# A four-layer graph network on one core: other instructions for the sorted neighbours' weighted sums and for the neighbour lists, one fused step in layer 1, and gathers tied to VectorE's progress

## Chip, core and metric

The kernel runs on one core of a Trainium2 chip, as one program. The metric is the device time of one execution in microseconds (us). The engines are named as in the profile: PE is TensorE, DVE is VectorE, ACT is ScalarE, POOL is GpSimd, and SP issues most of the DMAs.

## What is computed

Sixteen graphs of 1024 nodes, each with a 1024 x 1024 matrix `adj` of edge weights (about 1.6% of them nonzero) and 64 features per node, go through four residual layers. Each begins with a layer norm and a ReLU.

```python
h = max(layernorm(x), 0); x = x + (tanh([h, adj @ h] @ W1 + b1) @ W2 + b2)     # layer 0
h = max(layernorm(x), 0); num = (adj + I) @ h; den = rowsum(adj + I)           # layer 1
x = x + where(isnan(num / den), 0, num / den)
h = max(layernorm(x), 0); valid = dilated(adj) > 0                             # layer 2
agg[n, c] = sum over (tau, w) of w * quantile(h[valid[n], c], tau)             # tau .25 .5 .75
x = x + mask * (relu((h + agg) @ W1 + b1) @ W2)
h = max(layernorm(x), 0); x = x + ((adj @ h) / deg) @ Wn + h @ Ws + bias       # layer 3
```

Layer 2 is the hard one: for each node and each of the 64 features, three interpolated quantiles over the node's own ragged set of neighbours (some 10 to 38 of them).

## The kernel before

Everything is done graph by graph, with the 128 partitions holding nodes, eight blocks of 128 nodes per graph. Six Python generators, called streams, each walk over the 16 graphs and issue their instructions piece by piece:

- `adjacency`: loads `adj`, transposes it on PE, marks nonzero entries (L872, L874), takes out the dilated ones and writes for each node a row of keys to DRAM, 1024 minus the column for each neighbour and 0 elsewhere. It also sorts the nodes by how many neighbours they have. Ten of its PE and ACT steps wait for one another.
- `layers`: layers 0 and 1 and the layer norm of layer 2 (`messages` at L843 is the product `adj @ h` on PE, copied out by ACT at L844; layer 1's division is at L1118 to L1127).
- `neighbour_lists`: POOL loads the key rows of the nodes in order of their neighbour count (L1017, an indirect DMA). DVE takes the eight largest keys of each row with MAX8 (L1034), blanks them out with MATCH_REPLACE8 (L1037), takes the next eight, and so on: 22 MAX8 and 14 MATCH_REPLACE8 per graph. The found keys become the indices of the neighbours (L1043). It also works out weights `wts`, one for each sorted place of each node.
- `gathers`: for every place in a node's list POOL issues one indirect DMA that brings the 256-byte feature row of that neighbour (L1154), 152 of them per graph into five tiles `raw0` to `raw4`.
- `sorts`: DVE sorts the gathered rows place against place with a pruned network of minima and maxima between `raw` and a second tile `other` (L1190), then multiplies the places that can hold a quantile by their weights (L1207) and adds them with a strided reduction (L1211). The result `agg` goes to DRAM.
- `tail`: POOL brings `agg` back in the nodes' order (L1228), then the rest of layer 2 and layer 3 follow.

The eight blocks of nodes form five groups by neighbour count (`GROUPS`): two groups of one block with up to 38 and 20 places, and three groups of two blocks with up to 18, 16 and 13. The tiles `raw0` to `raw4` have one buffer each, so the gathers of a group for one graph start when the same group of the graph before is sorted. The lists run one graph ahead of the sorts.

The order of all instructions is written out by a planner: a variable `clk.dve` advances by a cost that the code states for each piece, each stream yields the time at which its next piece may start, and the loop takes the first stream that is due. Each engine executes its instructions in the resulting order. DVE counts its finished instructions in a semaphore. An instruction that nobody waits for leaves its count to a later one, so that a run of several sorting steps is posted by one addition at its last step.

Of the kernel before, what the change touches and what calls it, by code (L numbers as in the profile page):

```python
# [7 lines left out]
F32 = mybir.dt.float32  # L8
F16 = mybir.dt.float16
BF = mybir.dt.bfloat16  # L10
I32 = mybir.dt.int32
U16 = mybir.dt.uint16
# [6 lines left out]
C = 64  # L19
# [11 lines left out]
B_SW, B_SW2, B_LB, B_END = 0, 252, 504, 3576  # L31
H_ID, H_OFF, H_ONE, H_G, H_PI, H_END = 0, 128, 256, 384, 516, 1028

GROUPS = [(0, 1, 38, 17), (1, 1, 20, 15), (2, 2, 18, 12), (4, 2, 16, 10), (6, 2, 13, 1)]

E_ID, E_ONE, E_CAP, E_LOW, E_CN, E_Q, E_END = 0, 128, 256, 264, 272, 280, 320
J_ID, J_BIG, J_OFF, J_ST, J_ROW, J_ONE, J_PI, J_NI, J_END = 0, 128, 256, 384, 1408, 2432, 2560, 2688, 2696
KB = 4  # L40


# [665 lines left out]
def direct_path(ctx: ExitStack, tc: tile.TileContext, t: dict, out: bass.AP, flag):  # L708
# [24 lines left out]
    identf, onesf = cf[:, E_ID:E_ID + P], cf[:, E_ONE:E_ONE + P]  # L733
    cap8, low8, cn8 = (cf[:, e:e + NB] for e in (E_CAP, E_LOW, E_CN))
    identh, big_i, offdiag = (ch[:, e:e + P] for e in (J_ID, J_BIG, J_OFF))
    stair, pidx = ch[:, J_ST:J_ST + N], ch[:, J_PI:J_PI + P]
    nid = ch[:, J_NI:J_NI + NB]
    jrow, onerow = ch[0:1, J_ROW:J_ROW + N], ch[0:1, J_ONE:J_ONE + P]
    eps = const.tile([P, 1], F32, name="eps")
# [25 lines left out]
    w3n, w3s = weight("L3_gnn_W_neighbors", C), weight("L3_gnn_W_self", C)  # L765
    b3 = along("b3", t["L3_gnn_bias"])

    mask8 = const.tile([B * NB, P], U8, name="mask8")
    nc.gpsimd.dma_start(mask8, nodemask.rearrange("b (i p) -> (b i) p", p=P))
    maskf = const.tile([B * NB, P], F32, name="maskf")  # L770
    nc.vector.tensor_copy(maskf, mask8)
    pm = psum.tile([P, 512], F32, tag="t", name="pt", bufs=3)
    nc.tensor.transpose(pm[:, :B * NB], maskf, identf[:B * NB, :B * NB])
# [31 lines left out]
    def mid(u, shape):  # L805

        return work.tile(shape, F32, tag=f"mid{u}", name="mid", bufs=2)
# [38 lines left out]
    def per_node(p, lhs, w):  # L846

        for i in range(NB):
            nc.tensor.matmul(p[:, i * C:(i + 1) * C], lhs[:, i * P:(i + 1) * P], w, start=True, stop=True)  # L849
        return p.rearrange("p (i c) -> p i c", c=C)  # L850


    state = [dict() for _ in range(B)]
# [154 lines left out]
    def neighbour_lists(b):  # L1008


        g = state[b]
        ks = []

        def load_keys(i):
            if i < NB:
                k = lists.tile([P, N], F16, name="k", bufs=KB)
                nc.gpsimd.indirect_dma_start(k, None, g["keys_d"],  # L1017
                                             bass.IndirectOffsetOnAxis(ap=g["node"][:, i:i + 1], axis=0))
                clk.pool = max(clk.pool, clk.dve) + 1.3
                ks.append((k, clk.pool + 3.5))  # L1020

        for i in range(KB):
            load_keys(i)
        total = sum(n * -(-cap // 8) * 8 for _, n, cap, _ in GROUPS)
        found = lists.tile([P, total], F16, name="found", bufs=1)
        m = g["m"]
        o = 0
        for b0, n, cap, _ in GROUPS:
            for i in range(b0, b0 + n):
                src, at = ks[i]  # L1030
                yield at
                for r in range(-(-cap // 8)):
                    e = found[:, o:o + 8]
                    nc.vector.max(out=e, in_=src)  # L1034
                    clk.dve += 1.2
                    if (r + 1) * 8 < cap:
                        nc.vector.match_replace(out=src, in_to_replace=e, in_values=src, imm_value=0.0)  # L1037
                        clk.dve += 1.3
                    o += 8
                    yield clk.dve  # L1040
                load_keys(i + KB)
        index = lists.tile([P, total], I32, name="index")
        ts(index, found, -1.0, float(N), op0=ALU.mult, op1=ALU.add)  # L1043

        s = nodes.tile([P, 2, NB], F32, name="s")
        tt(s[:, 0], m, cap8, ALU.is_gt)
        tt(s[:, 1], m, low8, ALU.is_lt)
        tt(s[:, 0], s[:, 0], s[:, 1], ALU.max)
        tt(bad, bad, s[:, 0], ALU.max)

        at = nodes.tile([P, 3, NB], F32, name="at")
        for k in range(3):
            ts(at[:, k], m, (k + 1) / 4, -(k + 1) / 4, op0=ALU.mult, op1=ALU.add)
# [12 lines left out]
        g.update(index=index)  # L1066
        done.add(("index", b))
        yield after(1.7, act=1.7)
        wts = lists.tile([P, QT], F32, name="wts", bufs=3)
        tt(wts, far[:, 0], far[:, 2], ALU.add)  # L1070
        tt(wts, wts, far[:, 1], ALU.add)
        clk.dve += 0.4
        g.update(wts=wts)
        done.add(("lists", b))


    def layers(b):
# [39 lines left out]
        den = nodes.tile([P, NB, 1], F32, name="den")  # L1117
        ts(den, p[:, :, C:C + 1], 1.0, None, op0=ALU.add)  # L1118
        nc.vector.reciprocal(den, den)
        o, o1 = mid(0, [P, NB, C]), mid(0, [P, NB, C])  # L1120
        tt(o, p[:, :, :C], ha[:, :, :C], ALU.add)
        tt(o, o, den.to_broadcast([P, NB, C]), ALU.mult)

        ts(o1, o, 0.0, None, op0=ALU.max)
        ts(o, o, 0.0, None, op0=ALU.min)
        tt(o, o, o1, ALU.add)
        tt(x, x, o, ALU.add)  # L1127
        clk.dve += 3.8
        ha = nodes.tile([P, NB, C + 1], F32, name="h2", bufs=3)
        yield from preln(0, x, ha)  # L1130
        nc.sync.dma_start(h_ds[b % 3][:N].rearrange("(i p) c -> p i c", p=P), ha[:, :, :C])
# [10 lines left out]
    def gathers(b):  # L1142
        g = state[b]
        yield max(g["rows_at"], clk.pool)
        for k, (b0, n, cap, _) in enumerate(GROUPS):
            while not (b == 0 or ("sort", b - 1, k) in done):
                yield None
            raw = raws.tile([P, cap, n * C], F32, name=f"raw{k}")
            o = sum(c * -(-r // 8) * 8 for _, c, r, _ in GROUPS[:k])
            clk.pool = max(clk.pool, clk.dve)  # L1150
            for s in range(cap):
                for i in range(n):
                    at = o + i * -(-cap // 8) * 8 + s
                    nc.gpsimd.indirect_dma_start(raw[:, s, i * C:(i + 1) * C], None, h_ds[b % 3],  # L1154
                                                 bass.IndirectOffsetOnAxis(ap=g["index"][:, at:at + 1], axis=0))
                clk.pool += 1.27 * n
                if s % 4 == 3:
                    yield clk.pool - 3
            g[f"raw{k}"] = (raw, clk.pool + 4)
            done.add(("gather", b, k))  # L1160
        done.add(("gathers", b))


    def view(v, first, dims, w):

# [6 lines left out]
    def sorts(b):  # L1172
# [3 lines left out]
        for k, (b0, n, cap, low) in enumerate(GROUPS):  # L1176
# [20 lines left out]
            q = hi + 1 - lo  # L1197
            o = sum((_span(kk, ll)[1] + 1 - _span(kk, ll)[0]) * m for _, m, kk, ll in GROUPS[:k])
            wv = g["wts"][:, o:o + q * n].rearrange("p (q i) -> p q i", i=n)
            for (s, _, i, j), dims in result:  # L1200
                (c, d, _), outer = dims[-1], dims[0] if len(dims) > 1 else (1, 0, 0)
                d = max(d, 1)
                for r in range(outer[0]):
                    fr, to = i + r * outer[1], j + r * outer[1]
                    for ii in range(n):
                        cols = slice(ii * C, (ii + 1) * C)
                        tt(raw[:, fr:fr + (c - 1) * d + 1:d, cols], two[s][:, fr:fr + (c - 1) * d + 1:d, cols],  # L1207
                           wv[:, to:to + (c - 1) * d + 1:d, ii:ii + 1].to_broadcast([P, c, C]), ALU.mult)
                        clk.dve += 0.085 + c * C / 960
                        yield clk.dve  # L1210
            nc.vector.tensor_reduce(agg[:, b0:b0 + n].rearrange("p i c -> p (i c)"),  # L1211
                                    raw[:, lo:hi + 1].rearrange("p q w -> p w q"), AX.X, ALU.add)
            clk.dve += 0.085 + q * w / 960
            done.add(("sort", b, k))
            yield clk.dve
        yield clk.dve + 2
# [99 lines left out]
    with tc.manual_schedule():  # L1316
        ready = [0.0] * len(streams)
        while streams:

            soonest = None  # L1320
            for k, at in enumerate(ready):
                if at is not None and at > clk.dve:
                    soonest = at if soonest is None else min(at, soonest)
                    continue
                said = next(streams[k], -1.0)
                if said == -1.0:
                    del streams[k], ready[k]
                    break
                ready[k] = said
                if said is not None:  # L1330
                    break
            else:
                assert soonest is not None
                clk.dve = soonest
# [19 lines left out]
def _constants():  # L1354
# [14 lines left out]
    eh[p, J_BIG + p] = 2048  # L1369
    eh[:, J_OFF:J_OFF + P] = 1  # L1370
    eh[p, J_OFF + p] = 0
    eh[:, J_ST:J_ST + N] = p[:, None] < np.arange(N)
    eh[p, J_ST + p] = 2050
    eh[0, J_ROW:J_ROW + N] = -1024 - np.arange(N)
    eh[0, J_ONE:J_ONE + P] = 1
# [76 lines left out]
```

## Time and profile before

| | |
|---|---|
| median of 9 executions | 5327.71 us (5291.95 to 5380.86) |
| the profiled execution: its time, its span | 5354.12 us, 5352.3 us |
| granted TensorE clock | 0.637 |
| DVE busy | 3641.1 us, 68% of the span, 8698 instructions |
| POOL busy | 2830.9 us, 53%, 2707 instructions |
| PE busy | 2170.4 us, 41% |
| ACT busy | 1413.8 us, 26% |
| DMA | 372.65 MB, of which 117.88 MB by POOL's indirect DMAs |

Busy time says how long an engine had an instruction in it. On DVE independent instructions overlap a little, so the sum over instructions is larger than the time that they take in a row; start-to-start times from the timeline are the safer measure. In the waits "remote" and "issue" mark idle time for whose end the profile names no instruction.

### The profile page before, as it was taken

How to read it: one execution, taken by the hardware profiler on the slowest of the kernel's cores; microseconds unless marked ns; L12 is line 12 of the kernel's file. 1: busy time of each engine (PE TensorE's matmuls, PEld its weight loads, DVE VectorE, ACT ScalarE, POOL GpSimd, SP SyncE). 2: the span in 40 equal slices, each digit the busy share in tenths (PEclk: the TensorE clock that was granted, in tenths of full speed). 3: DMA queues.
4: the chain of work that ended last, by engine and by line, in shares of the span. 5: the costliest groups of instructions: out<-in, count | busy, mean ns of one | idle time of the engine just before them, and what ended most of it. 6: DMA issues, size and time to landing. Idle time of an engine off the chain costs nothing.

```text
span 5352.3 us, 33205 instructions
## 1 busy us (share of the span) xinstructions
PE 2170.4 (41%) x8387; PEld 1024.2 (19%) x8387; DVE 3641.1 (68%) x8698; ACT 1413.8 (26%) x2594; POOL 2830.9 (53%) x2707
## 2 busy tenths in 40 slices
PE   6443215444343435534344443434434353552022
PEld 3221112121211212121121211112121221211011
DVE  2445768756766677766767776776877766776755
ACT  5332213222322223232222322222232322321000
POOL 0436365664566566545655465564546555554740
PEclk8666656666565666656666666666766666665555
DMA  3322323332333434233332334333233432423221
GB/s 101 64 82 47 70 55 71 93 58 63 85 63 81 69 78 84 49 86 64 85 67 49 102 56 98 63 81 67 64 91 56 98 61 67 65 55 71 42 43 40
DMA packets 251851, 372.65 MB, mean 70 GB/s; under 512 B 120160, under 2 KB 120352, under 8 KB 251648
## 3 DMA queue, kind: packets, MB, share of 16 engines
q0 software_dynamic: 92640, 117.88, 18.3%
q1 hardware_dynamic: 158864, 251.87, 14.0%
q8 instruction: 68, 1.11, 0.1%
q14 instruction: 135, 1.11, 0.1%
q10 hardware_dynamic: 144, 0.69, 0.0%
HBM read 256.97 MB, written 113.25 MB: 69 GB/s over the span
## 4 chain that ended last, share of the span: by engine, by line
DVE 42%; another core or an unknown queue 27%; issue 12%; PE 10%; ACT 7%; DMA 2%; POOL 0%; SPq 0%; DVEq 0%; ACTq 0%; POOLq 0%
DVE other L1190 11%; DVE raw L1190 10%; DVE found L1034 6%; DVE k L1037 4%; DVE raw L1207 2%; PE pt L843 2%; PE pt L849 1%; ACT nb L885 1%; ACT nb L954 1%; PE tm L1272 1%; DVE agg L1211 1%; DVE nb L872 1%; PE pt L920 1%; ACT pt L956 1%
## 5 line engine op out<-in xcount | busy, mean ns | idle before, releaser
L1154 POOL DMA_INDIRECT raw<-h_d,index x2432 | 2540.5, 1045 | 1453.8 <-issue 724.4
L1190 DVE TENSOR_TENSOR other<-raw 128x128 f32<-128x128 f32 (+7 forms) x1488 | 764.4, 532 | 164.7 <-remote 104.3
L1190 DVE TENSOR_TENSOR raw<-other 128x256 f32<-128x256 f32 (+10 forms) x1424 | 676.7, 489 | 26.1 <-remote 12.7
L843 PE MATMUL pt<-adjt,ha 128*65 128x512 f32 (+1 forms) x1024 | 495.1, 646 | 281.6 <-DVE ha L1102 143.0
L1272 PE MATMUL tm<-at,ha 128*64 128x512 f32 x512 | 322.2, 744 | 512.0 <-DMA at<-adjt_d 444.0
L879 PE MATMUL pt<-ef,a 128*128 128x128 f32 x1024 | 245.1, 406 | 667.3 <-ACT adjt L880 403.7
L1017 POOL DMA_INDIRECT k<-keys_d,node x128 | 138.2, 1080 | 635.6 <-DVE node L1002 395.4
L1034 DVE MAX8 found<-k 128x8 f16<-128x1024 f16 x352 | 423.2, 1221 | 11.0 <-DMA k<-keys_d,node 3.3
L954 ACT ACTIVATE nb<-pt 128x1024 f16<-128x1024 f32 x128 | 130.8, 1022 | 1077.2 <-remote 646.8
L1228 POOL DMA_INDIRECT res<-agg_d,pos x128 | 142.8, 1115 | 370.9 <-DMA agg_d<-agg 318.1
L879 PEld LDWEIGHTS pt<-ef,a 128*128 128x128 f32 x1024 | 183.3, 211 | 721.9 <-ACT adjt L880 433.9
L1190 DVE TENSOR_TENSOR raw<-other,raw 128x128 f32<-128x128 f32 (+5 forms) x560 | 195.5, 355 | 159.9 <-remote 109.5
L1211 DVE TENSOR_REDUCE agg<-raw 128x64 f32<-128x1600 f32 (+4 forms) x80 | 194.1, 2426 | 144.0 <-remote 102.6
L1190 DVE TENSOR_TENSOR other<-raw,other 128x256 f32<-128x256 f32 (+4 forms) x592 | 206.2, 353 | 102.6 <-remote 68.3
L920 PE MATMUL pt<-eh,nbt 128*128 128x512 f16 (+3 forms) x1024 | 210.9, 363 | 150.5 <-ACT nbt L909 109.6
L1037 DVE MATCH_REPLACE8 k<-found,k 128x1024 f16<-128x1024 f16 x224 | 270.7, 1209 | 0.0
L843 PEld LDWEIGHTS pt<-adjt,ha 128*65 128x65 f32 (+1 forms) x1024 | 150.2, 150 | 607.5 <-issue 578.9
L880 ACT COPY adjt<-pt 128x512 f32<-128x512 f32 x256 | 138.2, 581 | 311.4 <-remote 257.1
L885 ACT ACTIVATE nb<-nb 128x512 f16<-128x512 f16 x256 | 159.7, 629 | 216.1 <-DVE nb L874 109.0
L844 ACT COPY big<-pt 64x1024 f32<-64x1024 f32 (+1 forms) x32 | 32.2, 1007 | 694.1 <-remote 356.1
L925 ACT ACTIVATE ab<-pt,sf 128x512 f16<-128x512 f32 x256 | 162.8, 691 | 199.2 <-DVE gone L930 54.3
L832 PE MATMUL pt<-ef,res 128*64 128x128 f32 x128 | 30.2, 416 | 444.5 <-DVE res L1232 305.0
(148 smaller groups left out, 4043.7 us busy)
## 6 DMA issues: line engine op xcount, KB each, us to landing
a<-in_adj_dram SPq DMA_DIRECT2D x128, 512.0 KB
adjt_d<-adjt SPq DMA_DIRECT2D x128, 512.0 KB
at<-adjt_d SPq DMA_DIRECT2D x256, 256.0 KB
raw<-h_d,index POOLq DMA_INDIRECT x2432
keys_d<-nb SPq DMA_DIRECT2D x128, 256.0 KB
x<-in_x_dram SPq DMA_DIRECT2D x16, 256.0 KB
h_d<-h SPq DMA_DIRECT2D x16, 256.0 KB
agg_d<-agg SPq DMA_DIRECT2D x16, 256.0 KB
```

Of the source, the lines that this page charges most:

```text
L843: nc.tensor.matmul(p[p0:p0 + n, s], h[:, j, :n], adjt[:, j, s], start=j == 0, stop=j == NB - 1)
L879: nc.tensor.transpose(p[:, u * P:(u + 1) * P], a[:, j * P:(j + 1) * P], identf)
L885: act(nb[:, i, s], nb[:, i, s], AF.Copy, accum_out=mn[:, q, i:i + 1])
L920: nc.tensor.matmul(p[:, o:e], nbt[:, j, :], stair[:, :e - o], start=j % 4 == 0, stop=j % 4 == 3)
L925: act(ab[:, s], p[:, s], AF.Abs, bias=sf[:, 2 + q, i:i + 1], scale=2.0)
L954: act(nb[:, i, :], p, AF.Relu)
L1034: nc.vector.max(out=e, in_=src)
L1037: nc.vector.match_replace(out=src, in_to_replace=e, in_values=src, imm_value=0.0)
L1154: nc.gpsimd.indirect_dma_start(raw[:, s, i * C:(i + 1) * C], None, h_ds[b % 3], bass.IndirectOffsetOnAxis(ap=g["index"][:, at:at + 1], axi ...
L1190: tt(to, v0, v1, ALU.max if greater else ALU.min)
L1211: nc.vector.tensor_reduce(agg[:, b0:b0 + n].rearrange("p i c -> p (i c)"), raw[:, lo:hi + 1].rearrange("p q w -> p w q"), AX.X, ALU.add)
L1272: nc.tensor.matmul(p[:C, :], ha[:, j, :C], ats[k], start=j == 0, stop=j == NB - 1)
```

## The change

1. **Weighted sums** (`sorts`). The products into `raw` and the strided reduction go. Each place is added by one `scalar_tensor_tensor` on 128 x 64 elements, `sum = place * weight + sum`, in a chain. A group of two blocks has two sums anyway; a group of one block keeps two by turns (`agg` and `half`) and adds them at the end. Neighbouring instructions of a chain are thus independent and each one needs the one before the last.
2. **Lists** (`neighbour_lists`). MATCH_REPLACE8 goes. After the first eight keys the row is rewritten as 16-bit integers less the least key found. Keys already found are then zero or positive and the rest are negative, and read as unsigned numbers the negative ones are the largest. MAX8 on that reading gives the next eight, and a small instruction turns them back into keys.
3. **Layer 1**: the four steps that clear NaNs and add become two fused ones.
4. **Gathers**: a new function `mark`, called at every turn of the planner's loop, lets DVE write a one-element tile if over 4 us of `clk.dve` have passed since the last mark. A new function `gate`, called before every fourth place of a gather, lets POOL copy the latest mark that no gate has read, and so wait until DVE got there. The tiles have eight buffers in turn, so a mark also waits until the gate that read the mark eight before it has run.
5. The planner's costs follow; a constant `stair` is halved and two tiles share memory, which changes no instruction but the constant's load.

```diff
-    mask8 = const.tile([B * NB, P], U8, name="mask8")
+    mask8 = lists.tile([B * NB, P], U8, tag="ab", name="mask8")
...
+    marks = []
+    def mark():
+        if not marks or clk.dve > marks[-1][0] + 4.0:
+            t = nodes.tile([1, 1], F32, name="mark", bufs=8)
+            nc.vector.memset(t, 0.0)
+            clk.dve += 0.06
+            marks.append((clk.dve, t))
+            del marks[:-2]
+    def gate():
+        if marks and len(marks[-1]) == 2:
+            t = nodes.tile([1, 1], F32, name="gate", bufs=2)
+            nc.gpsimd.tensor_copy(t, marks[-1][1])
+            marks[-1] += (True,)
...
-                for r in range(-(-cap // 8)):
-                    e = found[:, o:o + 8]
-                    nc.vector.max(out=e, in_=src)
-                    clk.dve += 1.2
-                    if (r + 1) * 8 < cap:
-                        nc.vector.match_replace(out=src, in_to_replace=e, in_values=src, imm_value=0.0)
-                        clk.dve += 1.3
+                nc.vector.max(out=found[:, o:o + 8], in_=src)
+                clk.dve += 1.15
+                yield clk.dve
+                less, before = src.bitcast(I16), None
+                for r in range(1, -(-cap // 8)):
+                    least = found[:, o + 7:o + 8]
+                    if r == 1:
+                        ts(less, src, least, None, op0=ALU.subtract)
+                    else:
+                        ts(less, less, before, least, op0=ALU.add, op1=ALU.subtract)
+                    before = least
+                    most = nodes.tile([P, 8], U16, name="most")
+                    nc.vector.max(out=most, in_=less.bitcast(U16))
                     o += 8
+                    ts(found[:, o:o + 8], most.bitcast(I16), 0.0, least, op0=ALU.min, op1=ALU.add)
+                    clk.dve += 1.8
                     yield clk.dve
...
-        ts(o1, o, 0.0, None, op0=ALU.max)
-        ts(o, o, 0.0, None, op0=ALU.min)
-        tt(o, o, o1, ALU.add)
-        tt(x, x, o, ALU.add)
-        clk.dve += 3.8
+        nc.vector.scalar_tensor_tensor(x, o, 0.0, x, op0=ALU.max, op1=ALU.add)
+        nc.vector.scalar_tensor_tensor(x, o, 0.0, x, op0=ALU.min, op1=ALU.add)
+        clk.dve += 2.4
...
             for s in range(cap):
+                if s % 4 == 0:
+                    gate()
...
+            places = []
             for (s, _, i, j), dims in result:
-                (c, d, _), outer = dims[-1], dims[0] if len(dims) > 1 else (1, 0, 0)
-                d = max(d, 1)
-                for r in range(outer[0]):
-                    fr, to = i + r * outer[1], j + r * outer[1]
-                    for ii in range(n):
-                        cols = slice(ii * C, (ii + 1) * C)
-                        tt(raw[:, fr:fr + (c - 1) * d + 1:d, cols], two[s][:, fr:fr + (c - 1) * d + 1:d, cols],
-                           wv[:, to:to + (c - 1) * d + 1:d, ii:ii + 1].to_broadcast([P, c, C]), ALU.mult)
...
-            nc.vector.tensor_reduce(agg[:, b0:b0 + n].rearrange("p i c -> p (i c)"),
-                                    raw[:, lo:hi + 1].rearrange("p q w -> p w q"), AX.X, ALU.add)
+                places += [(s, i + u, j + u) for u in sum_set(dims)]
+            half = nodes.tile([P, C], F32, name="half")
+            sums = [agg[:, b0 + ii] for ii in range(n)] if n == 2 else [agg[:, b0], half]
+            for e, (s, i, j) in enumerate(places):
+                for ii in range(n):
+                    v, wq = two[s][:, i, ii * C:(ii + 1) * C], wv[:, j, ii:ii + 1]
+                    to = sums[ii if n == 2 else e % 2]
+                    if e < 3 - n:
+                        ts(to, v, wq, None, op0=ALU.mult)
+                    else:
+                        nc.vector.scalar_tensor_tensor(to, v, wq, to, op0=ALU.mult, op1=ALU.add)
+                    clk.dve += 0.14
+                yield clk.dve
+            if n == 1:
+                tt(agg[:, b0], agg[:, b0], half, ALU.add)
...
         while streams:
+            mark()
             soonest = None
```

The changed program's own lists of instructions show the counts. For the sums, 832 products and 80 reductions before stand against 1504 fused multiply-adds, 160 first products and 32 final additions after. For the lists, 224 MATCH_REPLACE8 before stand against 224 row rewrites of 128 x 1024 and 224 small instructions of 128 x 8 after; MAX8 stays at 352. New are 806 marks on DVE and 413 gates on POOL. PE and ACT keep their instructions, and POOL its 2688 indirect DMAs.

More of the change, by code (lines that the diff above doesn't have):

```diff
@@ L32 @@
 H_ID, H_OFF, H_ONE, H_G, H_PI, H_END = 0, 128, 256, 384, 516, 1028
+I16 = mybir.dt.int16
 GROUPS = [(0, 1, 38, 17), (1, 1, 20, 15), (2, 2, 18, 12), (4, 2, 16, 10), (6, 2, 13, 1)]
 E_ID, E_ONE, E_CAP, E_LOW, E_CN, E_Q, E_END = 0, 128, 256, 264, 272, 280, 320
-J_ID, J_BIG, J_OFF, J_ST, J_ROW, J_ONE, J_PI, J_NI, J_END = 0, 128, 256, 384, 1408, 2432, 2560, 2688, 2696
+J_ID, J_BIG, J_OFF, J_ST, J_ROW, J_ONE, J_PI, J_NI, J_END = 0, 128, 256, 384, 896, 1920, 2048, 2176, 2184
 KB = 4
@@ L735, in direct_path @@
     identh, big_i, offdiag = (ch[:, e:e + P] for e in (J_ID, J_BIG, J_OFF))
-    stair, pidx = ch[:, J_ST:J_ST + N], ch[:, J_PI:J_PI + P]
+    stair, pidx = ch[:, J_ST:J_ST + N // 2], ch[:, J_PI:J_PI + P]
     nid = ch[:, J_NI:J_NI + NB]
@@ L766, in direct_path @@
     b3 = along("b3", t["L3_gnn_bias"])
-    mask8 = const.tile([B * NB, P], U8, name="mask8")
+    mask8 = lists.tile([B * NB, P], U8, tag="ab", name="mask8")
     nc.gpsimd.dma_start(mask8, nodemask.rearrange("b (i p) -> (b i) p", p=P))
-    maskf = const.tile([B * NB, P], F32, name="maskf")
+    maskf = lists.tile([B * NB, P], F32, tag="ab", name="maskf")
     nc.vector.tensor_copy(maskf, mask8)
@@ L1024, in neighbour_lists @@
         total = sum(n * -(-cap // 8) * 8 for _, n, cap, _ in GROUPS)
-        found = lists.tile([P, total], F16, name="found", bufs=1)
+        found = lists.tile([P, total], F32, name="found", bufs=1)
         m = g["m"]
@@ L1031, in neighbour_lists @@
                 yield at
-                for r in range(-(-cap // 8)):
-                    e = found[:, o:o + 8]
-                    nc.vector.max(out=e, in_=src)
-                    clk.dve += 1.2
-                    if (r + 1) * 8 < cap:
-                        nc.vector.match_replace(out=src, in_to_replace=e, in_values=src, imm_value=0.0)
-                        clk.dve += 1.3
+                nc.vector.max(out=found[:, o:o + 8], in_=src)
[11 more added lines that the diff above has]
+                    nc.vector.max(out=most, in_=less.bitcast(U16))
                     o += 8
+                    ts(found[:, o:o + 8], most.bitcast(I16), 0.0, least, op0=ALU.min, op1=ALU.add)
+                    clk.dve += 1.8
                     yield clk.dve
+                o += 8
                 load_keys(i + KB)
@@ L1119, in layers @@
         nc.vector.reciprocal(den, den)
-        o, o1 = mid(0, [P, NB, C]), mid(0, [P, NB, C])
+        o = mid(0, [P, NB, C])
         tt(o, p[:, :, :C], ha[:, :, :C], ALU.add)
         tt(o, o, den.to_broadcast([P, NB, C]), ALU.mult)
-        ts(o1, o, 0.0, None, op0=ALU.max)
-        ts(o, o, 0.0, None, op0=ALU.min)
-        tt(o, o, o1, ALU.add)
-        tt(x, x, o, ALU.add)
-        clk.dve += 3.8
+        nc.vector.scalar_tensor_tensor(x, o, 0.0, x, op0=ALU.max, op1=ALU.add)
+        nc.vector.scalar_tensor_tensor(x, o, 0.0, x, op0=ALU.min, op1=ALU.add)
+        clk.dve += 2.4
         ha = nodes.tile([P, NB, C + 1], F32, name="h2", bufs=3)
@@ L1161, in gathers, with sum_set @@
         done.add(("gathers", b))
+    def sum_set(dims):
+        offsets = [0]
+        for c, d, _ in dims:
+            offsets = [o + d * k for o in offsets for k in range(c)]
+        return offsets
     def view(v, first, dims, w):
@@ L1199, in sorts @@
             wv = g["wts"][:, o:o + q * n].rearrange("p (q i) -> p q i", i=n)
+            places = []
             for (s, _, i, j), dims in result:
-                (c, d, _), outer = dims[-1], dims[0] if len(dims) > 1 else (1, 0, 0)
-                d = max(d, 1)
-                for r in range(outer[0]):
-                    fr, to = i + r * outer[1], j + r * outer[1]
-                    for ii in range(n):
-                        cols = slice(ii * C, (ii + 1) * C)
-                        tt(raw[:, fr:fr + (c - 1) * d + 1:d, cols], two[s][:, fr:fr + (c - 1) * d + 1:d, cols],
-                           wv[:, to:to + (c - 1) * d + 1:d, ii:ii + 1].to_broadcast([P, c, C]), ALU.mult)
-                        clk.dve += 0.085 + c * C / 960
-                        yield clk.dve
-            nc.vector.tensor_reduce(agg[:, b0:b0 + n].rearrange("p i c -> p (i c)"),
-                                    raw[:, lo:hi + 1].rearrange("p q w -> p w q"), AX.X, ALU.add)
-            clk.dve += 0.085 + q * w / 960
+                places += [(s, i + u, j + u) for u in sum_set(dims)]
[13 more added lines that the diff above has]
+                tt(agg[:, b0], agg[:, b0], half, ALU.add)
+                clk.dve += 0.14
             done.add(("sort", b, k))
@@ L1371, in _constants @@
     eh[p, J_OFF + p] = 0
-    eh[:, J_ST:J_ST + N] = p[:, None] < np.arange(N)
+    eh[:, J_ST:J_ST + N // 2] = p[:, None] < np.arange(N // 2)
     eh[p, J_ST + p] = 2050
```

## The prediction

> **What bounds the kernel now.** I read the page's busy times and chain first, then the timeline where DVE stands still, then groups by form for prices.
>
> ```profile
> PE 2170.4 (41%) x8387; PEld 1024.2 (19%) x8387; DVE 3641.1 (68%) x8698; ACT 1413.8 (26%) x2594; POOL 2830.9 (53%) x2707
> ...
> DVE 42%; another core or an unknown queue 27%; issue 12%; PE 10%; ACT 7%; DMA 2%; POOL 0%; SPq 0%; DVEq 0%; ACTq 0%; POOLq 0%
> ```
>
> DVE carries most of the path, but 39% of it is idle time with no named end. The timeline of DVE shows such a time:
>
> ```profile
> 2104.59 0.49 DVE L1207 TENSOR_TENSOR raw<-raw,wts 128x128 f32<-128x128 f32 x2
> 2105.00 0.31 DVE L1207 TENSOR_TENSOR raw<-other,wts 128x128 f32<-128x128 f32 x1
> 2105.23 0.21 DVE L1207 TENSOR_TENSOR raw<-raw,wts 128x64 f32<-128x64 f32 x1
> 2111.76 1.59 DVE L1211 TENSOR_REDUCE agg<-raw 128x64 f32<-128x832 f32 x1 [6.31 <-issue]
> ```
>
> The reduction waits only for DVE's own products, which end at 2105.44, and starts 6.31 us later. On ACT, in another place:
>
> ```profile
> 2304.74 1.01 ACT L844 COPY big<-pt 65x1024 f32<-65x1024 f32 x1 [48.53 <-remote]
> ```
>
> PE's matmuls for it (L843, from 2258.18 for 16.56 us) end at 2274.7; the copy starts 30 us later. Meanwhile POOL issues gathers without a break. Busy times by stage (columns: stretch, its length, then PE, PEld, DVE, ACT, POOL):
>
> ```profile
> 2056.00:2080.00 24.00, 16.82 (x105) 12.33 (x106) 23.59 (x94) 12.28 (x18) 0.00 (x0) 0.72 0.18 73
> 2124.00:2162.00 38.00, 6.79 (x19) 1.56 (x19) 12.85 (x37) 2.05 (x3) 26.41 (x28) 0.54 0.49 46
> 2272.00:2304.00 32.00, 2.75 (x7) 0.69 (x5) 2.79 (x3) 0.00 (x0) 19.66 (x21) 0.58 0.28 22
> ```
>
> Without gathers DVE is busy 23.59 of 24 us; late in a run of gathers, 12.85 of 38. Over the whole trace I took DVE waits of over 0.4 us that name DVE's own count alone: 238, 695 us, POOL issuing in 91% of it (68% overall). Joined with the amount that the awaited instruction posts: more than 40 us into a run of gathers, 161 waits for a post of one unit lose 0.30 us each, 46 for three 2.05, 21 for six 4.96, 9 for nine or more 7.3. With no gathers, 72 waits for nine to twelve units lose 0.05. ACT's waits for PE posts of 15 units behave alike: 14.5 us each at 20 to 40 us into a run (42 waits), 0.18 without gathers (25). So a post of several units arrives late while POOL gathers without pause, the later in the run and the larger the post, the worse. POOL's runs last up to 82 us.
>
> A graph takes 312 us (first group's reduction from 507 in graph 0 to 5182 in graph 15, over 15), and 507 + 170 = 677 us lie outside. Per graph DVE is busy 228 us and POOL needs 227: 2821 us of indirect DMAs and 2688 gaps of 0.30 between them, over 16.
>
> **The change part by part**, prices from these rows:
>
> ```profile
> L1034 DVE MAX8 found<-k 128x8 f16<-128x1024 f16 x352 | 423.2, 1221 | 11.0 <-DMA k<-keys_d,node 3.3 <-issue 1.5 <-DVE k L1037 1.5
> L1037 DVE MATCH_REPLACE8 k<-found,k 128x1024 f16<-128x1024 f16 x224 | 270.7, 1209 | 0.0
> L930 DVE TENSOR_SCALAR gone<-ab,sf 128x1024 f16<-128x1024 f16 x112 | 54.2, 485 | 58.7 <-ACT ab L925 57.3 <-issue 1.4
> L1190 DVE TENSOR_TENSOR raw<-other 128x64 f32<-128x64 f32 x240 | 52.6, 219 | 3.6 <-issue 3.6
> ```
>
> *Lists.* MAX8 to MAX8 over a MATCH_REPLACE8 is 2.58 us (2000.68 to 2003.26). A round becomes a rewrite at L930's price (same shape, 16 bits, a scalar from a tile), 0.485, a MAX8, 1.22, and an eight-column step, 0.17 (L815), each with the 0.035 us that a dependent instruction starts late: 1.99. 224 x 0.59 = 132 us less. Bounds: the rewrite at the 1.22 of a full-rate instruction makes it 31 us more; at 0.43 (L1124), 144 less. MAX8 from 16-bit integers isn't in the trace; I keep 1.22, since the row has the same width, up to 1.42 (L1190 with 1216 columns).
>
> *Sums.* Products start 0.20, 0.27 or 0.14 us apart by width: 608 x 0.20 + 112 x 0.27 + 112 x 0.14 = 168. Reductions: 194 less overlap of 80 x 0.08 = 188. After: 1696 instructions of 64 columns. Independent ones start 0.137 apart though each takes 0.219; a dependent pair takes 0.254. Each link needs the last but one, so two fit in 0.254 to 0.274. A multiply-add with two SBUF tensors and a scalar isn't in the trace at this width; between 0.127 and 0.254 I take 0.15, near the independent row: 254. Net 356 - 254 = 102 less (141 less to 75 more). The waits go too: every link posts one unit, and L1211's and L1207's own waits for large posts, 142 + 56 = 198 us, vanish; a link that follows a late post loses some 0.3 us, so I keep 160 of the 198.
>
> [...]
>
> *Layer 1.* 0.43 + 0.46 + 0.70 + 0.69 and four gaps become two of 0.73: 16 x 0.9 = 14 less.
>
> *Marks.* 806 small writes at 0.08 (a MEMSET at 2257.97, the next instruction at 2258.05) = 64 more; bounds 0 and 160 (0.2 as a dependent one). A mark that waits for a gate holds all of DVE behind it, and with it every engine that waits for DVE; POOL would have to be eight marks, over 32 planned us, behind. The plan keeps them together, so I take nothing.
>
> *Gates.* 413, 26 per graph. POOL's in-order queue holds the gathers, L1017 and L1228 behind each; DVE's sorts wait for the gathers. Own cost between 0.1 (a POOL MEMSET) and 1.35 (a gather with its gap); I take 0.4, a MEMSET and a gap: 10 us, so POOL needs 237 per graph. The wait for the mark is meant to bind: when DVE or PE stands still, POOL stops after 4 to 8 gathers (5 to 10 us) rather than after up to 60.
>
> [...]
>
> *Sum.* DVE work -132 - 102 - 14 + 64 = -184, 12 per graph: 216. Of the 84 us of a graph in which DVE is not busy (312 - 228), 43 are own waits: 10 go with the sums, and I let short runs halve the other 33, to 16. The other 41 are waits for PE, ACT and loads, a good part late posts: 27 stay. New is DVE waiting for gathers that come just in time, 10. 216 + 16 + 27 + 10 = 269, above POOL's 237. The ends of the run lose 32 (shorter lists, sorts, sums): 645 + 15 x 269 = 4680 us of profiled time. That execution was 5354.1 against a median of 5327.7, so scaled by 0.995: 4655. Next late after this is POOL.
>
> **Rivals.**
>
> 1. *Gates do not shorten the runs* (POOL never gets ahead, so no gate binds). For it: POOL's 237 is close to DVE's need, and a pause of 0.7 us at 2265 did not help the reduction at 2274, 9.6 us late. Then only 12 + 10 per graph go: 645 + 15 x 290 = 4995, scaled 4970. Chance 0.24.
> 2. *Links don't overlap*: each costs 0.254, 175 us more DVE, 11 per graph: 4845, scaled 4820. For it: each waits for a semaphore; against: the spacing of independent rows, and the gap of two. [...] Chance 0.11. The rewrites at full rate give nearly the same (164 more, 4815), chance 0.04.
> 3. *Slower: gates serialize POOL with DVE.* Each gate waits for a mark planned up to 4 us back while DVE waits for the gather behind it. POOL has 312 - 227 = 85 us per graph, over 26 gates 3.3 us; beyond that it is late for DVE. At 4.5 us a graph is 344, 677 + 15 x 344 = 5837, scaled 5810; at 3.5 it is 318, 5420. Against it: POOL waited 705 us for sorts, so it was early. Chance 0.09.
> 4. *It balances out*, gains spent on gates: 5330, chance 0.03.
>
> **How the numbers follow.** The forecast has 0.49; with rivals 1 and 2, 0.88 for faster by over 0.5%, which is about what a measurement can tell from no change; 0.03 within it, 0.09 slower. The likeliest is 4655. Range: rival 1 with its savings only three quarters on the path is 312 - 16 = 296 per graph, 5060, and with the marks' upper bound about 5160. Below, POOL's floor of 237 gives 645 + 15 x 237 = 4200. So 4250 to 5180.
>
> **What would show it.** Right: no MATCH_REPLACE8; rewrites near 0.49; links starting about 0.15 apart; DVE's own waits below 400 us; ACT's L844 copy starting soon after PE; runs without a POOL pause below 40 us. Wrong: links 0.25 apart; POOL rows of L868 with idle time of several us each while DVE waits for `raw`; marks waiting for POOL.

## The result and the profile after

The changed kernel takes 4587.76 us (median of 10 runs) against 5331.19 us (31 runs): ratio 0.862, 95% interval 0.859 to 0.865. The forecast was 4655 us, in a range from 4250 to 5180. All further numbers depend on the chip: the kernel before takes 5263 to 5354 us on three of the five chips of the experiments and, with the same program, 4183 to 4209 us on the other two. I call them late and prompt chips, for what the traces show there. Each chip was used in one session only, so a property of the chip and a condition of the session are not told apart. The profiles of before and after above and below, "before" and "after" from here on, are of the late kind. A ratio is taken over the runs within 1.5% of the fastest of the same kernel, so it can differ a little from the ratio of the two medians beside it.

The page of after, busy times and chain:

```profile
PE 2115.0 (46%) x8387; PEld 1010.1 (22%) x8387; DVE 3510.1 (77%) x10256; ACT 1412.9 (31%) x2594; POOL 3014.4 (66%) x3120
...
DVE 45%; another core or an unknown queue 18%; PE 11%; issue 9%; ACT 7%; DMA 5%; POOL 4%; SPq 0%; DVEq 0%; ACTq 0%; POOLq 0%
```

DVE has 131 us less work, yet the span fell by 792 us, from 5352.3 to 4560.3: the time came out of idle stretches. Idle time without a named end on the chain (unknown and issue) went from 39% to 27%, and POOL is busy 66%, not 53%. The same table of stretches shows it where POOL gathers nearly all the time (columns as before):

```profile
2100.00:2150.00 50.00, 10.69 (x36) 4.48 (x37) 43.86 (x129) 17.72 (x32) 39.92 (x42) 0.50 0.46 47
2150.00:2200.00 50.00, 32.24 (x79) 10.97 (x78) 45.31 (x101) 6.57 (x9) 39.56 (x44) 0.79 0.28 56
```

DVE works 44 to 45 of 50 us beside 40 us of gathers; before, in a stretch late in a run of gathers, it worked 12.85 of 38. What POOL waits for, first a line of before, then two of after (us in total, times, longest):

```profile
POOL raw L1154 <- DVE agg L1211: 705.4, 29, 50.3
```
```profile
POOL raw L1184 <- issue: 673.5, 2344, 2.0
POOL gate L868 <- DVE mark L860: 494.4, 69, 16.8
```

Before, POOL waited 705 us at 29 places for the sums; now it waits 494 us at 69 gates, in shorter pieces. The groups that carry the new prices:

```profile
L1184 POOL DMA_INDIRECT raw<-h_d,index x2432 | 2587.1, 1064 | 699.9 <-issue 673.5
...
L1065 DVE MAX8 most<-k 128x8 uint16<-128x1024 uint16 x224 | 275.1, 1228 | 11.4 <-DVE k L1060 2.2
```

And a list of two rounds on DVE's timeline (start, length, line):

```profile
1950.23 1.22 DVE L1051 MAX8 found<-k 128x8 f32<-128x1024 f16 x1
...
1951.49 0.49 DVE L1060 TENSOR_SCALAR k<-k,found 128x1024 int16<-128x1024 f16 x1
1952.01 1.23 DVE L1065 MAX8 most<-k 128x8 uint16<-128x1024 uint16 x1
1953.28 0.23 DVE L1067 TENSOR_SCALAR found<-most,found 128x8 f32<-128x8 int16 x1
```

The second MAX8 starts 1.78 us after the first, where a round took 2.58. Late posts shrank but did not end: DVE's own waits are 259 us at 209 places (695 at 238 before), and ACT's waits of over 0.3 us on PE posts that were already due sum to 788 us (1389 before). In the waits of ACT, L846 (L844 before) still shows 291.8 us of unknown origin at 10 places, the longest 30.8 us (before: 356.1 us at 9).

### The profile page after: what moved, and what is told of

Same layout as the page of the kernel before. It is cut to its first block, busy times and chain, and to the rows that moved or that the text cites. A ratio compares the mean times of both kernels' runs of the same rounds, so it can differ in the third digit from the quotient of the medians.

```text
span 4560.3 us, 35608 instructions
## 1 busy us (share of the span) xinstructions
PE 2115.0 (46%) x8387; PEld 1010.1 (22%) x8387; DVE 3510.1 (77%) x10256; ACT 1412.9 (31%) x2594; POOL 3014.4 (66%) x3120
## 4 chain that ended last, share of the span: by engine, by line
DVE 45%; another core or an unknown queue 18%; PE 11%; issue 9%; ACT 7%; DMA 5%; POOL 4%; SPq 0%; DVEq 0%; ACTq 0%; POOLq 0%
DVE other L1227 12%; DVE raw L1227 11%; DVE most L1065 4%; DVE agg L1250 3%; POOL raw L1184 3%; DVE found L1051 2%; PE tm L1314 2%; PE pt L845 1%; PE pt L851 1%; DMA raw<-h_d,index 1%; DVE half L1250 1%; ACT nb L904 1%; DMA k<-keys_d,node 1%; PE pt L1281 1%
## 5 line engine op out<-in xcount | busy, mean ns | idle before, releaser
L1184 POOL DMA_INDIRECT raw<-h_d,index x2432 | 2587.1, 1064 | 699.9 <-issue 673.5
L868 POOL COPY gate<-mark 1x1 f32<-1x1 f32 x413 | 135.1, 327 | 521.7 <-DVE mark L860 494.4
L939 PE MATMUL pt<-eh,nbt 128*128 128x512 f16 (+3 forms) x1024 | 231.1, 389 | 324.6 <-ACT nbt L928 214.3
L1314 PE MATMUL tm<-at,ha 128*64 128x512 f32 x512 | 296.3, 701 | 62.3 <-DMA at<-adjt_d 52.6
L1065 DVE MAX8 most<-k 128x8 uint16<-128x1024 uint16 x224 | 275.1, 1228 | 11.4 <-DVE k L1060 2.2
L846 ACT COPY big<-pt 64x1024 f32<-64x1024 f32 (+1 forms) x32 | 32.2, 1008 | 617.8 <-remote 291.8
L949 DVE TENSOR_SCALAR gone<-ab,sf 128x1024 f16<-128x1024 f16 x112 | 56.0, 500 | 200.5 <-ACT ab L944 182.5
L939 PEld LDWEIGHTS <-nbt 128*128 128x128 f16 x1024 | 110.2, 122 | 436.5 <-ACT nbt L928 225.2
L1227 DVE TENSOR_TENSOR raw<-raw,other 128x256 f32<-128x256 f32 (+3 forms) x608 | 202.2, 337 | 4.8 <-issue 4.4
```

Source lines behind the costliest of these rows:

```text
L868: nc.gpsimd.tensor_copy(t, marks[-1][1])
L939: nc.tensor.matmul(p[:, o:e], nbt[:, j, :], stair[:, :e - o], start=j % 4 == 0, stop=j % 4 == 3)
L1065: nc.vector.max(out=most, in_=less.bitcast(U16))
L1227: tt(to, v0, v1, ALU.max if greater else ALU.min)
L1314: nc.tensor.matmul(p[:C, :], ha[:, j, :C], ats[k], start=j == 0, stop=j == NB - 1)
```

## The experiments

Theory A is the prediction's: posts come late while POOL gathers without a break, and the gates end that. Theory B: cheaper lists and sums made the difference. One caution holds for most of the runs: marks and the costs of the pieces move the planner's clock, so an edit that adds or drops them also changes the order of the instructions. Without marks and gates, only 4148 of DVE's 9450 other instructions stand at the same place in the sequence as in after.

**The kernel before with marks and gates alone** (first on a prompt chip, later on a late one; two small constant tiles share other buffers to make room).

```
+    marks = [] ... def mark() ... def gate()      (as in the kernel after)
             for s in range(cap):
+                if s % 4 == 0:
+                    gate()
...
+            mark()
             soonest = None
```

> The kernel before with the marks and gates alone; products, strided sums and MATCH_REPLACE8 stay. Theory A (posts of several units come late while POOL issues gathers without a break, and the gates end that): DVE's own waits over 0.4 us fall from 695 us to below 350, POOL's 1.0 us waits for sorts vanish into gates, and the time is 4720 to 4920 us. Theory B (the time comes from cheaper lists and sums, gates only cost): 5340 to 5420 us with own waits still above 600.

Measured on a prompt chip: 4282.34 us against 4208.65, ratio 1.018 (1.015 to 1.022). Neither theory had this, since both took 5331 us for granted. The waits of POOL there:

```profile
POOL raw L1173 <- issue: 625.6, 2226, 1.3
POOL gate L866 <- DVE mark L858: 201.2, 18, 18.7
```

DVE's own waits over 0.4 us are 3 us in all, so there is nothing to gain, and POOL is held 201 us at 18 marks. This fits the slower rival, with a price of under 2%. But before its sorts DVE waits only 13 us for gathered rows there; it waits 225 us for the key rows, which POOL loads in the same queue (185 us in the kernel before on the other prompt chip).

> The kernel before with marks and gates alone, again. Where before takes about 5300 us, after is 0.862 of before, and after without marks and gates 1.043, so the gates are worth 0.18 there on top of the chains and lists. If the gates' worth is their own (posts come through sooner, whatever the DVE work is), this is 0.82 to 0.88 of before: 4350 to 4700 us, since chains and lists together cost 0.04 there. If the gates only mend what the chains' many single posts broke, it is 0.95 to 1.02. Where before takes about 4200 us: 1.018 as before.

Measured on a late chip: 4690.18 us against 5263.4, ratio 0.900 (0.895 to 0.904). Every one of its runs is over 500 us below every run of before. The gates gain 10% by themselves, a little less than expected; the chains and lists add 4% on top (0.862 / 0.900 = 0.958).

**The kernel after without marks and gates**, on both kinds of chip.

```
-                if s % 4 == 0:
-                    gate()
...
-            mark()
```

> The kernel after without marks and gates. Theory A: own waits of DVE and ACT's waits for PE are back near those of before, except those of the wide reductions, which the chains no longer have: 4950 to 5150 us. Theory B: 64 us of marks less on DVE and no waits of POOL, 4480 to 4560 us.

On a prompt chip: 4061.5 us, ratio 0.965 (0.962 to 0.969).

> The kernel after without marks and gates again. Where before takes about 4200 us it showed 0.965 of before, and after itself 0.975, so here 0.965 again: the gates cost some 40 us. Where before takes 5331 us, theory A (gates end late posts) says 4950 to 5150 us, above after's 4588, and theory B (the chains and lists alone moved the late posts) 4500 to 4620 us.

On a late chip: 5575.86 us against 5353.96, ratio 1.043 (1.037 to 1.048). So on late chips marks and gates are worth 0.18 of before's time in the changed kernel, and without them the changed DVE work makes it slower. (On the same chip, the changed kernel with gates and with other numbers of sums, shown below, takes 4535.2 us.) Sums and lists were not run one by one on a late chip, so which of them does this is not known. Theory B has fallen there; theory A's number was too small by some 500 us. Its chain, and the waits of ACT and of POOL with it:

```profile
DVE 46%; another core or an unknown queue 28%; issue 11%; PE 7%; ACT 5%; DMA 1%; POOL 1%; DVEq 0%; ACTq 0%; POOLq 0%
```
```profile
ACT nbt L928 <- remote: 478.6, 29, 51.4
```
```profile
POOL raw L1182 <- DVE agg L1248: 263.4, 11, 71.2
```

ACT's copies after PE (`nbt`) now lose up to 51 us at a time. POOL waits for the sums 263 us at 11 places, not 705 at 29: pauses that had cut POOL's runs are gone. Gathers in runs of over 80 us (no pause over 0.8) sum to 2179 us, against 613 before and 514 after. How much DVE works in such runs, by the time since the run began (in brackets the time spent over 80 us into a run):

```
                             0 to 20   20 to 40   40 to 80   over 80 us
before                         85%       64%        41%        1% (53 us)
after without gates            91%       66%        41%       20% (899 us)
gates that wait for nothing    93%       80%        45%       11% (381 us)
after                          89%       81%        67%       59% (114 us)
before, prompt chip            91%       92%        82%       91% (2076 us)
```

On late chips DVE works less the longer the run lasts, and without gates 899 us are spent where it works a fifth of the time. In after a gate stops POOL when DVE falls behind (494 us at 69 gates), so its long runs are those in which DVE kept up. This fits lateness that grows with the run and quicker sums that lengthen the runs; the length was not varied by itself, and on the prompt chip it does no harm.

**Gates that wait for nothing**: the same copies at the same places, and the instructions of all engines in the same order as in after. This is the only pair of kernels that differs in the waits alone.

```
-            nc.gpsimd.tensor_copy(t, marks[-1][1])
+            nc.gpsimd.tensor_copy(t, eps[0:1])
```

> The kernel after, where each gate copies a constant that was written at the start: the same 413 copies on POOL at the same places, the same marks on DVE, but no wait. Theory A1 (POOL has to stand still for the posts to come through): late posts are back, 4900 to 5100 us. Theory A2 (a plain POOL instruction between the gathers is enough): own waits stay below 320 us, POOL's 494 us of waits for marks are gone, 4540 to 4640 us.

On a prompt chip: 4080.33 us, ratio 0.970 (0.967 to 0.974), within A2, but without late posts it tells nothing of them.

> The kernel after again with the 413 copies between the gathers and the 806 marks, but each copy reads a constant and so waits for nothing. Where before takes about 5350 us, after takes 4588 and without gates and marks it takes 5576. Theory A1 (POOL must stand still until DVE has come as far as the mark, which keeps it from running ahead of the late posts): 5300 to 5650 us. Theory A2 (any other POOL instruction between the gathers lets posts through): 4400 to 4650 us, since POOL's 494 us of waits go. Where before takes about 4200 us: ratio 0.97 as before, and nothing is told apart.

On a late chip: 5202.34 us against 5296.09, ratio 0.985 (0.969 to 1.001), between the two theories' ranges. On the scale of before's time, copies that wait for nothing recover 0.06 of the 0.18, the waiting the other 0.12 (the three kernels ran on different late chips, each beside before). Its chain:

```profile
DVE 44%; another core or an unknown queue 23%; issue 14%; PE 10%; ACT 6%; DMA 3%; POOL 0%; SPq 0%; DVEq 0%; ACTq 0%; POOLq 0%
```

ACT's late PE posts are 1362 us there, almost before's 1389. So a plain instruction between the gathers does little for them; POOL standing still does most. Why the kernel with copies is a third of the way better than the one without gates stays open; the two also differ in the order of the instructions.

**A mark every 2 planned us and a gate every 2 places.**

```
-        if not marks or clk.dve > marks[-1][0] + 4.0:
+        if not marks or clk.dve > marks[-1][0] + 2.0:
...
-                if s % 4 == 0:
+                if s % 2 == 0:
```

> The kernel after with a mark every 2 planned us in place of 4 and a gate every 2 places, so nearly twice the marks. If late posts are nearly gone after already, it costs 800 marks at 0.08 less what lies in waits: 4600 to 4670 us. If more gates remove the late PE posts that are left (790 us summed over ACT's waits), 4450 to 4550 us.

4111.52 us, ratio 0.977 (0.973 to 0.980), on a prompt chip. The edit gave 639 more marks but only 416 gates instead of 413: the gathers' stream yields every four places, and a new mark can only be written in between, so a second gate finds no mark that is unread. The expectations were for a late chip and for more gates, so their question stays open; beside the 0.970 of copies without waits on that chip the run shows only a small cost of marks and waiting.

**Before and after themselves on a prompt chip**, for their profiles.

> The kernel before itself, for a profile beside the others. It took 5331 us where the comparison was made and 4209 us beside the four runs before this one. If late posts are what differs, a run near 4209 us has DVE's own waits over 0.4 us below 60 us in all (695 us in the profile shown), no idle time put down to an unknown queue in the chain, and gathers that start as close (1.25 us) as in the profile shown. If it is the clock (0.637 and 0.683), PE's busy time accounts for it: 2170 us against about 2050, that is at most 120 of the 1120 us.

4185.27 us. Page and chain:

```profile
PE 2050.4 (49%) x8387; PEld 988.3 (24%) x8387; DVE 3628.7 (87%) x8698; ACT 1413.4 (34%) x2594; POOL 2963.9 (71%) x2707
...
DVE 39%; POOL 30%; issue 11%; DMA 8%; PE 8%; ACT 3%; DVEq 0%; POOLq 0%; ACTq 0%; SPq 0%
```

The unknown queue is gone from the chain; DVE's busy time is the same within 13 us, PE's 120 us less at the higher clock (0.681 against 0.637). DVE's own waits are 3 us, and ACT's 67 waits for posts of 15 units more than 40 us into a run of gathers lose 0.04 us each, with gathers 1.25 us apart as on the late chip. DVE's waits of both kinds fell from 695 + 923 to 3 + 488 us, 1127 of the 1148 us between 5331 and 4183. So late posts and what hangs on them make the difference, and the clock little.

> The kernel after itself beside the kernel before. Where before takes 4209 us, there are no late posts to remove: gates cost what they cost in the kernel before, some 74 us, against 4062 without them: 4090 to 4160 us, ratio 0.97 to 0.99. Rival: gates cost nothing here either, 4040 to 4080 us. Where before takes 5331 us: 4588 us, ratio 0.86.

4080.86 us, ratio 0.975 (0.972 to 0.977). The gates cost about 1% there: the ratio is 0.965 without them, in another comparison.

**Each part of the DVE work alone, in the kernel before**, on that prompt chip (the edits in words).

```
-   products into raw, then tensor_reduce over raw          (b_sums)
+   places, sums and links as in the kernel after
-   max and match_replace on src                            (b_lists)
+   max, row rewrite, max of 16-bit integers, small step
```

> The kernel before with the chains of multiply-adds alone. Links start 0.196 us apart in the profile after, not 0.15, so the chains take 1696 x 0.196 = 332 us against 356: 24 us of DVE less. Where before takes 4209 us: 4170 to 4220 us; with links at the forecast's 0.15 it would be 4100. Where before takes 5331 us, the waits for the large posts of products and reductions (198 us) go as well: 5100 to 5200 us.

4111.99 us, ratio 0.983 (0.980 to 0.986): 71 us less, more than the 24 that 0.196 per link gave. DVE's busy time fell by 29 us only (3628.7 to 3599.3), and its waits of over 0.4 us for others by 62 (487 to 425); what made those fall is open.

> The kernel before with the new lists alone. A round is 2.11 us after and 2.58 before: 224 x 0.5 = 110 us of DVE less. Where before takes 4209 us and DVE is 85% busy: 4100 to 4150 us if DVE sets the pace, 4180 to 4210 if POOL's gathers do. Where before takes 5331 us: 5190 to 5260 us.

4087.16 us, ratio 0.976 (0.974 to 0.979): 96 us less, as expected if DVE set the pace. But where did it go? Busy time fell by 113 us (to 3516.1). Per graph the period (first group's sum from graph 0 to graph 15, over 15) fell from 242.1 to 239.7 only, 35 us in all; the other 70 us of the profiled span went at its ends. With the sums alone it fell to 236.5, 83 us in all. After's period is 237.8 there, and POOL's busy time with the gaps between its issues is 3034.2 + 628.0 + 37.3 + 28.6 = 3728 us, 233 per graph. So on prompt chips the steady part comes close to POOL's own need, and cheaper DVE work has little left to give.

**One, four and two sums by turns**, in the first group, the second, and the groups of two.

```
+            if k == 0:
+                sums = sums[:1]
+            if k == 1:
+                sums += [nodes.tile([P, C], F32, name=f"half{h}", bufs=1) for h in (2, 3)]
...
-                    to = sums[ii if n == 2 else e % 2]
+                    to = sums[ii if n == 2 else e % len(sums)]
```

> The kernel after with one sum in the first group's chains, four by turns in the second's, and two as before in the three groups of two. Links with two sums start 0.196 us apart and last 0.273. Theory C (an instruction's own length sets it, 0.273 less the 0.08 that products overlap): with four sums 0.196 again, with one 0.27 to 0.31. Theory D (the wait for the last but one link sets it): with four sums about 0.14, with one about 0.39. The time hardly moves: in both, 23 links per graph cost 2 to 4 us more with one sum and up to 1 less with four.

4535.2 us against 5353.96 on a late chip, ratio 0.849 (0.845 to 0.853): faster than both kernels, and below after's 0.862 from its own comparison. I take no cause from that. The timeline, first group with one sum, then second group with four:

```profile
2276.35 4.13 DVE L1254 SCALAR_TENSOR_TENSOR agg<-raw,wts,agg 128x64 f32<-128x64 f32 x13
...
3374.93 0.28 DVE L1254 SCALAR_TENSOR_TENSOR half<-other,wts,half 128x64 f32<-128x64 f32 x1
3375.13 0.47 DVE L1254 SCALAR_TENSOR_TENSOR half<-raw,wts,half 128x64 f32<-128x64 f32 x2
3375.52 0.28 DVE L1254 SCALAR_TENSOR_TENSOR agg<-raw,wts,agg 128x64 f32<-128x64 f32 x1
```

One sum: thirteen links in 4.13 us, (4.13 - 0.28) / 12 = 0.321 us apart. Four sums: 0.195 (3375.13 to 3375.52, two links). Two sums on after's timeline on the prompt chip:

```profile
2044.46 0.28 DVE L1250 SCALAR_TENSOR_TENSOR agg<-raw,wts,agg 128x64 f32<-128x64 f32 x1
2044.65 0.27 DVE L1250 SCALAR_TENSOR_TENSOR half<-raw,wts,half 128x64 f32<-128x64 f32 x1
2044.85 0.27 DVE L1250 SCALAR_TENSOR_TENSOR agg<-raw,wts,agg 128x64 f32<-128x64 f32 x1
```

Also 0.196 in the median. Theory D has fallen, and the spacing fits theory C, the link's own length less an overlap of 0.08; one sum is a little above theory C's 0.31. Two sums are enough, and are worth 0.125 us a link (0.321 against 0.196). With one sum a link of 0.28 starts 0.321 after the one before, so a gap of 0.04 lies between them; with two by turns no gap is seen.

## Why the prediction came out

Busy time and waits on the late chips, from the traces (columns: before, after, after without gates, gates that wait for nothing, gates alone; "late PE posts" is ACT's waits of over 0.3 us on posts that were due):

```
                          before  after  no gates  no waits  gates alone
ratio to before             1     0.862   1.043     0.985      0.900
us per graph              311.6   267.6   333.9     303.3      271.7
DVE's own waits > 0.4 us    695     259     322       379        218
DVE's other waits > 0.4     923     679    1659      1202        736
late PE posts, ACT         1389     788    1638      1362        529
```

*The sum.* A graph was to take 269 us and takes 267.6. The ends were to take 645 and take 4560.3 - 15 x 267.6 = 546: the first group's sum of graph 0 is done at 345 us instead of 507. Of the 120 us between 4680 and the span, 99 are this: I took only the cheaper work off the ends, but the late posts go from there too.

*Lists.* Forecast 132 less. From each instruction's start to the next one's, waits cut off, lists took 713 us (before, prompt chip) and take 601 (after without marks, prompt chip): 112 less. The busy time of the kernel with the new lists alone fell by 113. The rewrite's price held in the first round (0.493 against 0.485); the later form, on integers with two scalars, takes 0.570. MAX8 from 16-bit integers takes 1.228, as assumed.

*Sums.* Forecast 102 less. By the same count 366 against 338: 28 less, and the kernel with the chains alone has 29 us less busy time. The step that failed is "between 0.127 and 0.254 I take 0.15, near the independent row". The independent rows start 0.082 us before the one ahead has ended, and the link is longer (0.276, not 0.219), so the overlap already on record gives 0.276 - 0.082 = 0.194 as soon as the length is known. That price alone is 1696 x 0.046 = 78 us. Rival 2, links that do not overlap at 0.254 each, comes true only for one sum, where a link costs 0.321.

*Layer 1.* The two fused steps take 0.692 us each, where 0.73 was taken.

*Marks and gates.* 64 us for marks was wrong: in 57 cases on the prompt chip a link, a mark and a link take 0.198 us where two links take 0.196. A mark costs nothing there: DVE is busy 3476.5 us with the 806 marks and 3475.8 without. A gate's own cost is 1.399 - 1.257 = 0.14 us of POOL (medians from gather to gather with and without a copy that waits for nothing, late chip), not 0.4.

*Waits.* Own waits were put at 16 us per graph, and 259 / 16 is that; but they are 218 us with gates alone, so no gain of the chains shows on top. The others were put at 27 + 10 and are 679 / 16 = 42; the 10 for gathers that come just in time are 41 / 16 = 3. DVE's work, 216, is 3510 / 16 = 219.

*Luck.* The forecast is 1.5% above the result, but the terms are not that good: sums and lists gave 74 and 20 us less than forecast, while the marks cost 64 us less and the ends 99. These errors cancel in part.

*What each part would do.* This is where the reasoning failed although the total did not. Rival 1 (no help from the gates) was priced at 4970 us, with 160 us of own waits saved by the chains. Without gates the kernel takes 5576. Own waits did fall, 695 to 322, but DVE's waits for others rose from 923 to 1659. I priced the change in DVE's work with the lateness held fixed, and it was not: POOL's runs grew longer without gates, and DVE worked least late in them. That the quicker sums are what lengthened the runs is likely but not shown. The gains of gates and sums are not to be added: the gates are worth 10% alone and 17% after the chains and lists (0.862 / 1.043 = 0.826).

*Signs named in advance.* No MATCH_REPLACE8, rewrites near 0.49, own waits below 400 and no marks held by POOL all came. The copy at L844 (now L846) starting soon after PE came in part. Posts of 15 units that ACT takes 20 to 40 us into a run fell from 14.5 to 2.8 us late. Links at 0.15 and runs below 40 us did not: the runs without a pause have a median of 30 us, but a quarter are over 50 and the longest is 116 (before, by the same count: median 47, longest 102). So a gate bounds how far POOL runs ahead, not how long it runs.

*The slower rival* (gates serialize POOL) did not decide on late chips. Its sign, gates that hold POOL for several us each, did come (494 us at 69 gates), but DVE waits only 41 us for gathered rows. On prompt chips gates cost 1 to 2%.

## What to carry to other kernels

Where idle time follows no engine and no transfer, ask what was running beside it, and bound that engine's lead over the others before making the waiting work cheaper: work made cheaper elsewhere may lengthen the lead, as is likely here (1.043 of before without gates). Run both kernels on more than one chip before a cause is called a property of the hardware. Where an order is planned from costs, compare kernels that keep the order, as the copies without waits do. Price an instruction that overlaps the one before as its own length less the overlap of its nearest row (here 0.276 - 0.082), and use two accumulators by turns where one makes each link wait (0.321 against 0.196 us a link).

## What was not expected of the hardware

The same program loses 695 us to DVE's own waits on one chip and 3 us on another, with the same gathers at the same distance (1.25 us). What differs between the chips, or between the sessions, is not seen in any trace here. On the late chips it shows mostly while POOL issues indirect DMAs (91% of the 695 us), most of all for posts of several units (over 40 us into a run 7.3 us for nine or more, 0.30 for one), and a wait put into POOL's queue relieves it more than a plain copy does (0.862 against 0.985 of before).

The rows do not show the loss, only the time between them does: 20 to 40 us into a run of gathers, a post of 15 units from PE is awaited 0.04 us past the end of its row on the prompt chip (38 waits) and 14.5 us on the late one (42 waits), with rows of 0.24 and 0.26 us. DVE's own posts behave alike, with 3 and 695 us of waits. So the time goes between the end of the awaited row and the start of the row that waits; what passes in it is not shown.
